# A four-byte tile allocated behind the FFN weights instead of ahead of them

## The chip, the cores and the metric

The kernel runs on one core of a Trainium2 chip. The metric is the device time of one execution in microseconds. The core has a matrix engine (TensorE, PE in the profile, with its weight loads PEld shown apart), a vector engine (VectorE, DVE), a scalar engine (ScalarE, ACT), GpSimd (POOL) and SyncE (SP), which here issues most of the DMA transfers.

## The reference

A transformer layer in two halves on x of shape 4 x 512 x 512, with pre-normalisation and residuals. The first half is an attention that works in the Fourier domain of each of the 16 heads (32 values a head): normalised spectra, a running sum over the positions, a product, and the way back. The second half is a gated FFN (512 to 1536 to 512) whose weights are rounded to 8-bit floats and back.

```python
q = (x @ W_q.T).reshape(B, S, H, hd)
kv = (x @ W_kv.T).reshape(B, S, H, hd)
qf = _l2_normalize_complex(jnp.fft.fft(q, axis=-1))
kvf = _l2_normalize_complex(jnp.fft.fft(kv, axis=-1))
kvf = jnp.cumsum(kvf, axis=1)
values_hat = jnp.fft.ifft(qf * kvf, axis=-1).real
attn = values_hat.reshape(B, S, D) @ W_o.T
...
gate = jax.nn.silu(_quantized_matmul(x, gate_w, gate_scale))
up = _quantized_matmul(x, up_w, up_scale)
return _quantized_matmul(gate * up, down_w, down_scale)
...
x = x + attn_ref(_layernorm(x), W_q, W_kv, W_o)
x = x + ffn_ref(_layernorm(x), gate_w, up_w, down_w, gate_scale, up_scale, down_scale)
```

`_quantized_matmul` multiplies by the weights cast to float8_e4m3 and back, then by a scale.

## The kernel before

The order of every engine's instructions is the order in which the code records them. The work is staged in three.

At the start the attention weights are loaded (`raw`, on SP's queue) and multiplied by the tables of the transform, so that one product of x with the folded weights gives a spectrum: `fold_in` and `fold_out`, into `wkv`, `wq` and `wo`.

Then come 16 chunks of 128 positions, `for i in range(2, N)` with the first two written out ahead of it. A chunk's two spectra (`spectrum`, line 302, tiles `pq`) are f32 matmuls; each of these is two instructions in the profile. `squared` and `summed` (lines 313 and 318) and the power -0.5 on POOL (`norms`, line 323, operands `ss` and `nhalf`) give the norms. `k_scaled` and `k_low` split the scaled values into two fp32r tiles, `kh` and `kl`. The running sum is two fp32r matmuls with the triangle of ones `tri_r` as weights (`running`, line 357, tile `cum`). `products`, `combined`, `v_transpose` and `project` (line 397, tile `po`, f32, with the weights taken from `qvT`) end the chunk. `stats` has another power on POOL (line 259), of the tile `dev`. Between them, `next_parts` rounds the FFN's weights piece by piece; the last of a piece's operations, `quant_sub` (line 225), writes 128 x 1024 elements of `wg`, `wu` or `wd`.

The third stage is the FFN: 48 steps, four batches of 512 rows by 12 blocks of 128 inner columns. In a step, `inner` has 16 fp32r matmuls (line 465): `lhsT`, the weights loaded into the array, is a 128 x 128 block of `wg` or `wu`; `rhs`, streamed through it, is `yh` or `yl`, 512 columns. Their results are the tiles `gu`. ACT and DVE make `fh` and `fl` of them. `down` has 8 fp32r matmuls for an earlier step (line 498, tiles `pd`): here `fh` or `fl` is loaded and 512 columns of `wd` are streamed. In all that is 48 x 24 = 1152 matmuls. Each is preceded by its own load of weights, which the profile shows as LDWEIGHTS on PEld.

Constants lie in the pool `const`, one buffer each, and are placed in SBUF one behind the other in the order of their allocation, each in whole units of 32 bytes per partition. A tile of four bytes so takes 32. The addresses, in bytes within a partition, of the tiles around the change are:

| tile | bytes | address before | past a multiple of 64 |
|---|---|---|---|
| over | 4 | 18592 | 32 |
| table | 4 | 18624 | 0 |
| nhalf | 64 | 18656 | 32 |
| tri_r | 512 | 18720 | 32 |
| wg | 24576 | 19232 | 32 |
| wu | 24576 | 43808 | 32 |
| wd | 24576 | 68384 | 32 |
| gus | 96 | 92960 | 32 |
| dsc | 2048 | 93056 | 0 |

The other tiles lie behind these. All that are matmul operands there start on a multiple of 64: `yh`, `yl`, `fh`, `fl`, `kh`, `kl`, `xT`, `qvT`, `wq`, `wkv`, `wo`. Of the 128 x 1 tiles `less` and `dev`, some start on a multiple of 64 and some 32 bytes past one.

`table` is set to zero on POOL (line 131) and passed through a Silu on ACT (line 132), whose first instruction on ACT is a load of the activation table. Nothing reads `table` afterwards.

Of the kernel before, what the change touches and what calls it, by code (L numbers as in the profile page):

```python
# [7 lines left out]
F32 = mybir.dt.float32  # L8
I32 = mybir.dt.int32
F32R = mybir.dt.float32r  # L10
AF = mybir.ActivationFunctionType
# [4 lines left out]
P = 128  # L16
# [14 lines left out]
def tile_fft_attention_then_fp8_ffn(  # L31
# [38 lines left out]
    nc = tc.nc  # L70
# [9 lines left out]
    const = ctx.enter_context(tc.tile_pool(name="const", bufs=1))  # L80
# [45 lines left out]
    nc.gpsimd.memset(eps, EPS)  # L126
    over = const.tile([P, 1], F32, name="over")
    nc.gpsimd.memset(over, -E4M3_OVERFLOW * DOWN * HUGE)

    table = const.tile([P, 1], F32, name="table")  # L130
    nc.gpsimd.memset(table, 0.0)
    nc.scalar.activation(table, table, AF.Silu)
    nhalf = const.tile([P, H], F32, name="nhalf")
    nc.gpsimd.memset(nhalf, -0.5)
    tri_r = const.tile([P, P], F32R, name="tri_r")
# [1 line left out]
    wg = const.tile([P, KC, FF], F32R, name="wg")  # L137
    wu = const.tile([P, KC, FF], F32R, name="wu")
    wd = const.tile([P, MC, D], F32R, name="wd")
    y_all = dram.tile([B, TC, P, D], F32, name="y_all")  # L140
    xn_all = dram.tile([B, TC, P, D], F32, name="xn_all")

# [609 lines left out]
```

## Time and profile before

| what | us |
|---|---|
| median of 3 runs | 481.35 |
| lowest and highest run | 479.42, 481.39 |
| the profiled execution | 480.92 |
| its span, first to last instruction | 479.1 |
| PE busy | 466.3 |
| DVE busy | 286.4 |
| ACT busy | 214.9 |
| POOL busy | 200.9 |

The span is what the views of the profile divide up; the profiled execution's own time has 1.8 us more, which lie around it. Busy times of different engines overlap. Matmuls are pipelined: one shows some 0.39 us, but the next starts 0.23 us after it, so the cadence is read from the starts, or from the chain of work that ended last, which merges neighbours of one kind and gives the start, the length and the count.

A row of the groups reads: line, engine, operation, output<-inputs by their tiles (buffer numbers left out), shapes, count, busy us and mean ns of one, then idle time before them.

```profile
L465 PE MATMUL gu<-yh,wg 128*128 128x512 f32 x192 | 77.0, 401 | 0.0
...
L498 PE MATMUL pd<-wd,fl 128*128 128x512 f32 x192 | 75.7, 394 | 0.0
```

### The profile page before, as it was taken

Reading aid. Unit: us, or ns where it says so; the run is one execution under the profiler, and the core shown is the slowest. Engines: PE = TensorE matmul, PEld = TensorE weight load, DVE = VectorE, ACT = ScalarE, POOL = GpSimd, SP = SyncE. Lnnn points to the kernel's source line nnn. Section 1 sums busy time; section 2 is a strip of 40 time slices with the busy share of each in tenths; the row PEclk is TensorE's granted clock in tenths of the full one; section 3 lists DMA queues with packets and bytes.
Section 4 is the critical chain, followed back from the end, with each engine's and each line's share of the span. In section 5 each row is a group of like instructions: output and inputs, shape, how many; then the busy total and the mean of one; then the engine's idle time right before and its main releaser. Section 6 shows DMA issues by size and latency. Waiting matters only on the chain.

```text
span 479.1 us, 5013 instructions
## 1 busy us (share of the span) xinstructions
PE 466.3 (97%) x1736; PEld 313.7 (65%) x1736; DVE 286.4 (60%) x399; ACT 214.9 (45%) x418; POOL 200.9 (42%) x134
## 2 busy tenths in 40 slices
PE   6999999999999999999999999999999999999995
PEld 5534454444444445568888888888888888888883
DVE  1558998888998787768898352333433332522225
ACT  3647475655646864315753325533226433222220
POOL 0257999987897986531332140122210021400002
PEclk9999999999999999999999999999999999999999
DMA  8920424342442101424241040430041420200002
GB/s 288 349 66 23 154 86 134 110 148 87 140 154 68 64 22 35 164 91 150 55 100 22 1 175 2 100 77 0 22 155 36 96 46 0 89 0 1 0 0 88
DMA packets 46152, 40.72 MB, mean 85 GB/s; under 512 B 27696, under 2 KB 28080, under 8 KB 46128
## 3 DMA queue, kind: packets, MB, share of 16 engines
q1 hardware_dynamic: 45744, 40.39, 26.9%
q8 instruction: 13, 0.21, 0.2%
q14 instruction: 11, 0.09, 0.1%
q10 hardware_dynamic: 384, 0.03, 0.1%
HBM read 28.85 MB, written 11.53 MB: 84 GB/s over the span
## 4 chain that ended last, share of the span: by engine, by line
PE 77%; DVE 8%; ACT 5%; POOL 4%; DMA 3%; issue 2%; SPq 0%; DVEq 0%; ACTq 0%
PE gu L465 37%; PE pd L498 19%; PE pq L302 12%; PE po L397 6%; POOL rn L323 3%; DMA row<-end 2%; PE pkv L150 1%; PE pt_v L271 1%; ACT sq L313 1%; ACT end L364 1%; DVE ss L318 1%; DVE qm L217 1%; PE pw L165 1%; PE cum L357 1%; DVE qa L221 1%
## 5 line engine op out<-in xcount | busy, mean ns | idle before, releaser
L323 POOL TENSOR_TENSOR rn<-ss,nhalf 128x16 f32<-128x16 f32 x32 | 108.2, 3383 | 22.5 <-DVE ss L318 22.5
L478 DVE SCALAR_TENSOR_TENSOR f<-gu,gus,g 128x512 f32<-128x512 f32 x48 | 36.0, 750 | 114.4 <-PE gu L465 112.9
L465 PE MATMUL gu<-yh,wg 128*128 128x512 f32 x192 | 77.0, 401 | 0.0
L465 PE MATMUL gu<-yh,wu 128*128 128x512 f32 x192 | 76.2, 397 | 0.0
L465 PE MATMUL gu<-yl,wg 128*128 128x512 f32 x192 | 75.8, 395 | 0.0
L498 PE MATMUL pd<-wd,fl 128*128 128x512 f32 x192 | 75.7, 394 | 0.0
L498 PE MATMUL pd<-wd,fh 128*128 128x512 f32 x192 | 75.7, 394 | 0.0
L465 PE MATMUL gu<-yl,wu 128*128 128x512 f32 x192 | 75.7, 394 | 0.0
L481 ACT CAST fh<-f 128x512 fp32r<-128x512 f32 x48 | 29.8, 621 | 90.8 <-DVE f L478 90.8
L302 PE MATMUL pq<-wkv,xT 128*128 128x512 f32 x128 | 57.7, 594 | 0.8 <-DVE xT L294 0.8
L476 ACT ACTIVATE g<-gu,gus 128x512 f32<-128x512 f32 x48 | 33.0, 688 | 55.2 <-PE gu L465 55.2
L397 PE MATMUL po<-wo,qvT 128*128 128x512 f32 x128 | 57.6, 593 | 0.0
L302 PE MATMUL pq<-wq,xT 128*128 128x512 f32 x128 | 57.6, 592 | 0.0
L510 POOL TENSOR_TENSOR o<-o,ys 128x512 f32<-128x512 f32 x14 | 17.7, 1295 | 83.6 <-DVE o L508 83.6
L483 DVE TENSOR_TENSOR fl<-f,fh 128x512 fp32r<-128x512 f32 x48 | 36.2, 755 | 27.0 <-ACT fh L481 26.8
L302 PEld LDWEIGHTS pq<-wkv,xT 128*128 128x128 f32 x128 | 24.1, 190 | 30.6 <-issue 27.5
L465 PEld LDWEIGHTS gu<-yh,wg 128*128 128x128 f32 x192 | 36.0, 188 | 9.3 <-issue 0.5
L465 PEld LDWEIGHTS gu<-yl,wg 128*128 128x128 f32 x192 | 36.0, 188 | 9.2 <-issue 0.5
L498 PEld LDWEIGHTS pd<-wd,fh 128*128 128x128 f32 x192 | 36.0, 188 | 8.9
L498 PEld LDWEIGHTS pd<-wd,fl 128*128 128x128 f32 x192 | 36.0, 188 | 8.8 <-DVE fl L483 0.2
L465 PEld LDWEIGHTS gu<-yl,wu 128*128 128x128 f32 x192 | 36.1, 188 | 8.7
L465 PEld LDWEIGHTS gu<-yh,wu 128*128 128x128 f32 x192 | 36.0, 188 | 8.5
(84 smaller groups left out, 596.4 us busy)
## 6 DMA issues: line engine op xcount, KB each, us to landing
x<-in_x SPq DMA_DIRECT2D x16, 256.0 KB, 2.8
xT<-in_xT SPq DMA_DIRECT2D x16, 256.0 KB, 2.6
y_all<-x SPq DMA_DIRECT2D x16, 256.0 KB, 2.0
ys<-y_all SPq DMA_DIRECT2D x4, 1024.0 KB, 6.8
out<-o SPq DMA_DIRECT2D x16, 256.0 KB, 2.0
rawf<-in_gate_w SPq DMA_DIRECT2D x3, 1024.0 KB, 6.9
rawf<-in_up_w SPq DMA_DIRECT2D x3, 1024.0 KB, 5.4
rawf<-in_down_w SPq DMA_DIRECT2D x3, 1024.0 KB, 6.2
```

Of the source, the lines that this page charges most:

```text
L150: nc.tensor.matmul(pw[i][:, j * P : (j + 1) * P], lhsT=r[:, j, i * P : (i + 1) * P], rhs=fwd, start=True, stop=True,)
L165: nc.tensor.matmul(pw, lhsT=inv, rhs=r[:, j, :], start=True, stop=True)
L302: nc.tensor.matmul(pq, lhsT=xTs[i][:, k, :], rhs=w[:, k, :], start=k == 0, stop=k == KC - 1)
L323: nc.gpsimd.tensor_tensor(rns[i, j], sss.pop((i, j)), nhalf, ALU.pow)
L397: nc.tensor.matmul(po, lhsT=qvT[:, k, :], rhs=wo[:, k, :], start=k == 0, stop=k == KC - 1)
L465: nc.tensor.matmul(p, lhsT=w[:, k, m * P : (m + 1) * P], rhs=v[:, k, :], start=k == 0 and v is yhs[b], stop=k == KC - 1 and v is yls[b],)
L476: nc.scalar.activation(g, pgu[0], AF.Silu, scale=gus[:, 0, m : m + 1])
L478: nc.vector.scalar_tensor_tensor(f, pgu[1], gus[:, 1, m : m + 1], g, ALU.mult, ALU.mult)
L481: nc.scalar.copy(fh, f)
L483: nc.vector.tensor_tensor(fl, f, fh.bitcast(F32), ALU.subtract)
L498: nc.tensor.matmul(pds[b][c], lhsT=v[:, c * P : (c + 1) * P], rhs=wd[:, m, :], start=m == 0 and v is fused[n][0], stop=m == MC - 1 and v i ...
L510: add.tensor_tensor(o, o, ys[b][:, c, :], ALU.add)
```

## The change

The three lines of `table` move from ahead of `nhalf` to behind `wd`. Its 32 bytes are then taken behind the weights: `nhalf`, `tri_r`, `wg`, `wu` and `wd` start 32 bytes lower, at 18624, 18688, 19200, 43776 and 68352, each a multiple of 64. `table` starts at 92928, and `gus` and all that follows stay where they were. On POOL, the memset of `table` comes behind that of `nhalf`. The orders of PE, DVE, ACT and SP stay as they were, and no tile changes its size.

```diff
     over = const.tile([P, 1], F32, name="over")
     nc.gpsimd.memset(over, -E4M3_OVERFLOW * DOWN * HUGE)
+    nhalf = const.tile([P, H], F32, name="nhalf")
+    nc.gpsimd.memset(nhalf, -0.5)
+    tri_r = const.tile([P, P], F32R, name="tri_r")
+
+    wg = const.tile([P, KC, FF], F32R, name="wg")
+    wu = const.tile([P, KC, FF], F32R, name="wu")
+    wd = const.tile([P, MC, D], F32R, name="wd")
 
     table = const.tile([P, 1], F32, name="table")
     nc.gpsimd.memset(table, 0.0)
     nc.scalar.activation(table, table, AF.Silu)
-    nhalf = const.tile([P, H], F32, name="nhalf")
-    nc.gpsimd.memset(nhalf, -0.5)
-    tri_r = const.tile([P, P], F32R, name="tri_r")
-
-    wg = const.tile([P, KC, FF], F32R, name="wg")
-    wu = const.tile([P, KC, FF], F32R, name="wu")
-    wd = const.tile([P, MC, D], F32R, name="wd")
     y_all = dram.tile([B, TC, P, D], F32, name="y_all")
```

More of the change, by code (lines that the diff above doesn't have):

```diff
@@ L128, in tile_fft_attention_then_fp8_ffn @@
     nc.gpsimd.memset(over, -E4M3_OVERFLOW * DOWN * HUGE)
-    table = const.tile([P, 1], F32, name="table")
-    nc.gpsimd.memset(table, 0.0)
-    nc.scalar.activation(table, table, AF.Silu)
     nhalf = const.tile([P, H], F32, name="nhalf")
@@ L139, in tile_fft_attention_then_fp8_ffn @@
     wd = const.tile([P, MC, D], F32R, name="wd")
+    table = const.tile([P, 1], F32, name="table")
+    nc.gpsimd.memset(table, 0.0)
+    nc.scalar.activation(table, table, AF.Silu)
     y_all = dram.tile([B, TC, P, D], F32, name="y_all")
```

## The prediction

> **What bounds the kernel now.** I read the head of the page first, then busy time by stage, then the chain of work that ended last, and then single matmuls in order of time.
>
> ```profile
> span 479.1 us, 5013 instructions
> PE 466.3 (97%) x1736; PEld 313.7 (65%) x1736; DVE 286.4 (60%) x399; ACT 214.9 (45%) x418; POOL 200.9 (42%) x134
> PEclk9999999999999999999999999999999999999999
> PE 77%; DVE 8%; ACT 5%; POOL 4%; DMA 3%; issue 2%; SPq 0%; DVEq 0%; ACTq 0%
> ```
>
> ```profile
> 60.00:132.00 72.00, 72.00 (x200) 34.42 (x201) 64.53 (x92) 43.95 (x84) 63.07 (x33) 1.00 0.36 118
> ...
> 212.00:475.00 263.00, 261.42 (x1118) 209.33 (x1116) 120.45 (x159) 95.06 (x181) 48.86 (x44) 1.00 0.20 53
> ```
>
> The columns of the two stage rows are the stretch, its length, busy time (and count) of PE, PEld, DVE, ACT, POOL, the granted clock, DMA share and GB/s. From 212 to 475 us, the FFN, PE never rests at full clock while DVE is busy 120 of 263 us: the cadence of the FFN's matmuls is the time. The chain gives this cadence:
>
> ```profile
> 214.26 3.73 PE gu L465 x16
> ...
> 454.77 3.73 PE gu L465 x16
> 458.50 1.86 PE pd L498 x8
> 460.36 7.46 PE gu L465 x32
> ```
>
> From 214.26 to 460.36 lie 44 steps of 16 gu and 8 pd matmuls: 246.10 / (44 x 24) = 233.05 ns for each. All 1152 FFN matmuls are fp32r. A plain f32 one is issued as two instructions, 429 ns apart (eight pq matmuls in 3.43 us), which is 214.4 ns for 512 columns if each of the two runs over them twice (an estimate). So an fp32r matmul takes some 18.6 ns more than this f32 pace, and all of these, 1152 x 18.6 = 21.4 us, lie on the path.
>
> **The change part by part.** The bytes. wg, wu, wd and tri_r start 32 bytes past a multiple of 64 before, and on a multiple of 64 after; nhalf moves likewise. Each other operand of these matmuls (yh, yl, fh, fl, kh, kl) stands on a multiple of 64 in both. So before, gu loads shifted weights (wg, wu) and streams unshifted data (yh, yl), while pd loads unshifted weights (fh, fl) and streams shifted data (wd). Every fp32r matmul has exactly one shifted operand, which makes the 18.6 ns suspect: is this the price of the shift? Nothing runs the same matmul in the new place, so I bound it: -21.4 us if all of the excess goes; 0 if none; and upward by the longest step in the trace. The starts of FFN matmuls go in threes, 231, 232 and 237 to 238 ns; if all became the long one, (238 - 233.05) x 1152 = +5.7 us.
>
> Which end is nearest? The trace has stretches without the shift. While a matmul streams, the weights of the next one are loaded. A last gu matmul streams yl (unshifted) while fh (unshifted) is loaded: both operands stand as they will after the change. Likewise the second cum matmul streams kl while qvT is loaded, all unshifted; its own tri_r was loaded before.
>
> ```profile
> 120.80 0.40 PE L357 MATMUL cum<-kl,tri_r 128*128 128x512 f32 x1
> ...
> 121.04 1.02 PE L397 MATMUL po<-wo,qvT 128*128 128x512 f32 x2
> ```
>
> ```profile
> 301.49 0.39 PE L465 MATMUL gu<-yl,wu 128*128 128x512 f32 x1
> 301.73 0.39 PE L498 MATMUL pd<-wd,fh 128*128 128x512 f32 x1
> ...
> 303.36 0.39 PE L498 MATMUL pd<-wd,fl 128*128 128x512 f32 x1
> 303.58 0.39 PE L465 MATMUL gu<-yh,wg 128*128 128x512 f32 x1
> ```
>
> The first column is the start. From last gu to first pd is 0.24 us, from cum kl to po 0.24 us: not 0.215. By the start stamps in ns, the 46 undisturbed gu-to-pd steps have a mean of 230.8, the usual kl-to-po step is 233 to 235; and the opposite case, pd streams shifted wd while shifted wg is loaded, has 230.0 (44 steps). Besides, gu and pd swap the shifted role and keep the same threes. And a load of shifted tri_r begins 110 ns before the next load can, where unshifted transposes follow each other by 109. So fp32r runs at 230 to 238 ns with none, one or both operands shifted. I take 0, the nearest of the three values, and keep -21.4 and +5.7.
>
> [...]
>
> The tri_r matmuls: 32 of them, the same question, at most 32 x 18.6 = 0.6 us, partly under other limits; 0.
>
> The writes of wg, wu and wd (L225) move too, and nhalf, which POOL reads:
>
> ```profile
> L225 DVE SCALAR_TENSOR_TENSOR wg<-qm,qa x6: 1215/1216/1219, 41.3 to 230.0; 128x1024 fp32r<-128x1024 f32 x6
> ...
> L221 DVE SCALAR_TENSOR_TENSOR qa<-qm,rawf x18: 1209/1219/2201, 25.8 to 257.0; 128x1024 f32<-128x1024 f32 x18
> ...
> L323 POOL TENSOR_TENSOR rn<-ss,nhalf x32: 2902/3306/4156, 16.1 to 195.4; 128x16 f32<-128x16 f32 x32
> ```
>
> The three numbers are minimum, median and maximum in ns. A write to shifted wg has 1216 ns, the same form into unshifted qa 1219: 0 for the 18 writes; bounds by the minima, 6 ns x 18 = 0.1 us either way. For L323 the bounds are its own extremes: 32 x (2902 - 3383) = -15.4 us and 32 x (4156 - 3383) = +24.7 us of POOL time, but only 2.7% of the span (13 of 108 us) is on the chain, so -1.9 and +3.0 us. I take 0: the other power on POOL, L259, writes a dev that is shifted in some chunks and not in others, and its undisturbed executions take some 551 ns in both; the spread looks like waiting beside DVE.
>
> What else is moved: one memset on POOL and nothing on PE, DVE, SP or a DMA queue. On ACT the order stays (table load, then the activation on table).
>
> ```profile
> 0.72 1.28 ACT L132 ACT_TABLE_LOAD   x1 [0.72 <-PEq L739]
> ...
> 0.77 0.10 POOL L131 MEMSET table<- 128x1 f32 x1
> 0.80 0.11 POOL L134 MEMSET nhalf<- 128x16 f32 x1
> ...
> 2.01 0.20 ACT L132 ACTIVATE table<-table 128x1 f32<-128x1 f32 x1
> ```
>
> The memset of table now comes behind nhalf's, some 0.03 us later, and ends by 0.91; its reader on ACT starts at 2.01, held by the table load. That load hides it with 1.1 us to spare; without this cover it would cost 0.03 us, and ACT's next work waits until 5.56 for x anyway. Nhalf's first reader comes after 5 us.
>
> **Sum.** The profiled execution took 480.92 us: its span of 479.1 and 1.8 around it. Add 0: 480.9. The median shown is 481.35 with runs from 479.42 to 481.39; I give 481.1, between the two. The case's own range is 479.2 to 483.0, the spread of the runs and the same upward.
>
> **The rivals.**
> Faster, the whole excess: the shift costs all 18.6 ns, and one shifted operand suffices for it. For it: all rows at 214.4 ns have unshifted operands, all at 233 one shifted. Against: the stretches above; it lives only if reads run so far ahead that one step doesn't show the rate. 480.9 - 21.4 = 459.5 us.
>
> Faster, one line: if PE fetched 64 bytes at a time, a matmul would read 33 pieces of its 2048 shifted bytes and 8 of the 512 of weights, or 32 and 9: 41 in both roles, 40 after. That explains why gu and pd are alike. 233.05/41 x 1152 = 6.5 us: 474.4. Against: it wants 227 ns for the 46 unshifted steps and 239 for the 44 with two shifts; they have 230.8 and 230.0.
>
> Slower: weights and stream now begin on the same 64-byte phase, and the load of the next weights collides with the running stream in every matmul of the FFN loop, where the opposite phase let most pass. Price: every step becomes the long one, +5.7, 486.6 us; it decides from 2.1 ns a matmul (2.4 us) on. For it: the recurring long step shows that something does beat against the stream. Against: gu-to-pd and pd-to-gu steps have both operands on the same phase already and are not long. POOL's +3.0 by nhalf ends within this price and gets no chance of its own.
>
> That the change doesn't do what it says can be left out: the allocated addresses of the built program do move.
>
> **How the numbers follow.** No change, 0.42. Whole excess 0.20, one line 0.14, collision 0.24. The chances on both sides of no change are too large to leave either out, so the range goes to the whole excess below, 459.5, and the collision above, 486.6. The unchanged case has 0.01 of its chance beyond half a per cent on either side (0.5%, 2.4 us, is about what a measurement of this kernel can tell from no change). So faster 0.35, within 0.5% 0.40, slower 0.25.
>
> **What would show it.** Right: the step of 16 gu and 8 pd matmuls again takes 5.59 us in the chain, the threes of 231, 232 and 238 stay, L225 and L323 keep their minima. The whole excess: a step of 24 x 214.4 = 5.15 us. One line: 5.46. Collision: 5.7, at full clock. If the FFN loop is as before and the time differs, look at 60 to 201 us, where POOL is busy 63 of 72 us at first, and at L323. The prediction fails by its choice of 0 if those stretches are too short to show the rate of a stream.

## The result, and the profile after

| | before | after |
|---|---|---|
| median of 20 runs each, us | 480.79 | 479.76 |
| lowest and highest, us | 479.42, 481.97 | 478.49, 481.19 |
| span of the profiled execution, us | 479.1 | 477.8 |
| one FFN step (16 gu, 8 pd), ns | 5593.3 | 5573.4 |
| mean gap from gu, from pd, ns | 233.26, 232.63 | 232.97, 230.66 |

The ratio is 0.9982, with a 95% interval of 0.9973 to 0.9991: faster by 0.4 to 1.3 us. That is within the 0.5% that was called no change, but it is not nothing. A gap here and below is the time from the start of one matmul to the start of the next, by the start stamps of the trace in ns; a step is the time from the first gu matmul of one FFN step to that of the next; the steps are means over the undisturbed ones behind 214 us, the gaps over all undisturbed matmuls there, the last 24 of pd included.

The head of the page after the change, and its row of busy time by stage for the FFN:

```profile
span 477.8 us, 5013 instructions
PE 465.8 (98%) x1736; PEld 314.3 (66%) x1736; DVE 285.8 (60%) x399; ACT 214.8 (45%) x418; POOL 200.9 (42%) x134
PEclk9999999999999999999999999999999999999999
```

```profile
212.00:475.00 263.00, 260.00 (x1117) 209.11 (x1115) 121.11 (x159) 95.00 (x181) 49.31 (x43) 1.00 0.19 54
```

Nothing is busy for longer or shorter to speak of; the granted clock is 1.00 as before. PE's last matmul ends 1.4 us earlier, which is the 1.4 us that PE is less busy in this window (261.42 before). The chain shows where this comes from. Four steps from the middle of the FFN, before (first block) and after:

```profile
303.75 3.73 PE gu L465 x16
307.48 1.86 PE pd L498 x8
...
326.12 3.73 PE gu L465 x16
```

```profile
302.95 3.73 PE gu L465 x16
306.67 1.85 PE pd L498 x8
...
325.24 3.73 PE gu L465 x16
```

Before, 303.75 to 326.12 is 22.37 us; after, 302.95 to 325.24 is 22.29. So 0.020 us a step, three quarters of it in pd: by the stamps, the eight pd matmuls go from 1860.8 to 1845.7 ns and the sixteen of gu from 3732.5 to 3727.6. If all 48 steps gain the same (an estimate), that is 48 x 19.9 = 0.96 us: the measured difference of the medians, 1.03, to within its interval. Of the 1.4 us by which PE's last matmul ends earlier, 0.47 had been gained when the first full step began (214.26 before, 213.79 after), but kernels with the same FFN weights as the change began theirs at 213.59 and 214.05 (e1 and e4 below), so this part varies from run to run and is not the change's.

The row of gaps within gu changes too. Before, they went in threes; after, a matmul of `yh` is followed by a long gap and one of `yl` by a short one (means of 237.0 and 228.9 ns; before 233.7 and 232.8):

```profile
303.24 0.40 PE L465 MATMUL gu<-yh,wg 128*128 128x512 f32 x1
303.48 0.39 PE L465 MATMUL gu<-yl,wg 128*128 128x512 f32 x1
303.71 0.40 PE L465 MATMUL gu<-yh,wg 128*128 128x512 f32 x1
303.95 0.39 PE L465 MATMUL gu<-yl,wg 128*128 128x512 f32 x1
304.18 0.40 PE L465 MATMUL gu<-yh,wg 128*128 128x512 f32 x1
```

The other rows that were shown of before:

```profile
0.77 0.11 POOL L130 MEMSET nhalf<- 128x16 f32 x1
0.82 0.10 POOL L138 MEMSET table<- 128x1 f32 x1
```

```profile
0.72 1.28 ACT L139 ACT_TABLE_LOAD   x1 [0.72 <-PEq L739]
2.01 0.20 ACT L139 ACTIVATE table<-table 128x1 f32<-128x1 f32 x1
```

```profile
L225 DVE SCALAR_TENSOR_TENSOR wg<-qm,qa x6: 1214/1216/1219, 42.0 to 229.4; 128x1024 fp32r<-128x1024 f32 x6
...
L323 POOL TENSOR_TENSOR rn<-ss,nhalf x32: 2900/3288/4354, 16.8 to 195.9; 128x16 f32<-128x16 f32 x32
```

The memset of table starts 0.05 us later and its reader again at 2.01, behind the table load. The write of wg keeps its 1216 ns, and the power on POOL its minimum, 2900 against 2902.

### The profile page after: what moved, and what is told of

It reads as the page before. It is cut to its first block, busy times and chain, and to the rows that moved or that the text cites. A ratio compares the mean times of both kernels' runs of the same rounds, so it can differ in the third digit from the quotient of the medians.

```text
span 477.8 us, 5013 instructions
## 1 busy us (share of the span) xinstructions
PE 465.8 (98%) x1736; PEld 314.3 (66%) x1736; DVE 285.8 (60%) x399; ACT 214.8 (45%) x418; POOL 200.9 (42%) x134
## 4 chain that ended last, share of the span: by engine, by line
PE 77%; DVE 9%; ACT 5%; POOL 4%; DMA 3%; issue 2%; SPq 0%; DVEq 0%; ACTq 0%
PE gu L465 37%; PE pd L498 19%; PE pq L302 12%; PE po L397 6%; POOL rn L323 3%; DMA row<-end 2%; PE pkv L150 1%; PE pt_v L271 1%; ACT sq L313 1%; ACT end L364 1%; DVE ss L318 1%; DVE qm L217 1%; PE pw L165 1%; PE cum L357 1%; DVE qa L221 1%
```

## The experiments

For all of them it helps to write down one number for gu and one for pd: the distance, the address of the operand that is loaded less that of the operand that is streamed, modulo 512 bytes. 512 is the size of a loaded block of 128 columns, so within a loop the distance stays what it is while k, m and c run. Before, gu stands at 416 (wg at 19232, yh at 103296) and pd at 160 (fh at 187840, wd at 68384); after, at 384 and 192. Where no ratio is given below, a run's time is that of a single execution, and the argument goes by the steps.

| run | gu, pd at | gu, pd ns | step ns | in units of 6.667 ns | time us | before, beside it |
|---|---|---|---|---|---|---|
| before | 416, 160 | 233.3, 232.6 | 5593.3 | 839 | 480.79 |  |
| after | 384, 192 | 233.0, 230.7 | 5573.4 | 836 | 479.76 |  |
| e1 | 384, 192 | 233.0, 230.7 | 5573.4 | 836 | 480.15 | 481.01 |
| e2 | 384, 160 | 232.5, 232.5 | 5580.3 | 835 and 839 in turn | 480.03 | 481.01 |
| e3 | 352, 192 | 233.6, 230.8 | 5582.9 | 835 and 840 in turn | 480.48 | 481.01 |
| e4 | 384, 192 | 233.0, 230.7 | 5573.4 | 836 | 479.97 | 481.01 |
| e7 | 448, 128 | 229.2, 232.5 | 5526.9 | 829 | 477.30 | 481.65 |
| e8 | 0, 64 | 228.4, 233.1 | 5520.0 | 828 | 477.13 | 481.65 |
| e9 | 384, 0 | 232.5, 229.0 | 5553.3 | 833 | 478.88 | 480.67 |
| e10 | 0, 0 | 229.0, 231.1 | 5513.3 | 827 | 477.46 | 480.67 |
| e11 | 480, 480 | 233.3, 233.4 | 5600.0 | 840 | 480.85 | 480.67 |
| e12 | 0, 192 | 227.9, 229.3 | 5480.0 | 822 | 475.16 | 481.09 |

### e1: the same addresses by another tile

```diff
-    eps = const.tile([P, 1], F32, name="eps")
-    nc.gpsimd.memset(eps, EPS)
...
     wd = const.tile([P, MC, D], F32R, name="wd")
+    eps = const.tile([P, 1], F32, name="eps")
+    nc.gpsimd.memset(eps, EPS)
```

> The tile eps, also four bytes, is allocated and set behind the weights; table stays where it was. The weights, tri_r and nhalf lie at exactly the addresses of the change, while the memset of table stays ahead of nhalf's. Theory A (the addresses alone make the difference): the FFN step of 16 gu and 8 pd matmuls takes 5573 ns as after the change (5593 before), the gaps alternate in gu as after the change, and the time is 0.9 us under before. Theory B (the order of the memsets, or chance in the start of the kernel): 5593 ns, the time of before.

Measured: step 5573.4 ns, gaps as after the change, and 480.15 us against 481.01 of before measured beside it, ratio 0.9982 (0.9969 to 0.9995). The addresses make the whole difference in the step; the place of table's memset makes none.

### e2 and e3: the weights of gu alone, the data of pd alone

Both are shown against the kernel before.

```diff
-    table = const.tile([P, 1], F32, name="table")
-    nc.gpsimd.memset(table, 0.0)
-    nc.scalar.activation(table, table, AF.Silu)
...
+    table = const.tile([P, 1], F32, name="table")
+    nc.gpsimd.memset(table, 0.0)
+    nc.scalar.activation(table, table, AF.Silu)
     wd = const.tile([P, MC, D], F32R, name="wd")
```

> table is allocated between wu and wd: wg and wu (loaded as weights) at a multiple of 64, wd (streamed) 32 past one as before. Theory A1 (the place of the streamed operand counts): gu as after or before (233.0 against 233.3 ns), pd stays at 232.6 ns, step 5588 to 5593 ns. Theory A2 (the place of the loaded weights counts, and pd profits from gu's): pd falls to 230.7 ns without having moved itself, step 5573 ns.

```diff
-    eps = const.tile([P, 1], F32, name="eps")
-    nc.gpsimd.memset(eps, EPS)
-    over = const.tile([P, 1], F32, name="over")
-    nc.gpsimd.memset(over, -E4M3_OVERFLOW * DOWN * HUGE)
...
+    over = const.tile([P, 1], F32, name="over")
+    nc.gpsimd.memset(over, -E4M3_OVERFLOW * DOWN * HUGE)
     wd = const.tile([P, MC, D], F32R, name="wd")
+    eps = const.tile([P, 1], F32, name="eps")
+    nc.gpsimd.memset(eps, EPS)
```

> over is allocated between wu and wd and eps behind wd: wg and wu 32 past a multiple of 64, wd at one. Theory A1 (the place of the streamed operand counts): pd falls from 232.6 to 230.7 ns, gu stays at 233.3 with its threes of 231, 232 and 238; step 5577 ns. Theory A2: pd stays at 232.6, step 5588 to 5593 ns.

Measured: with wd as before, pd keeps 232.5 ns; with wd as after, it falls to 230.8. So pd's gain belongs to wd, which is A1 for pd, and A2 falls. But gu moves a little by itself in both (232.5 and 233.6 ns), and the steps of 5580.3 and 5582.9 ns lie between the expectations: two kinds of step alternate, 5568 and 5592 ns in e2, 5566 and 5600 in e3. So one group's gaps seem to depend on what lies around it. By its addresses e3 isn't quite the half that it was meant to be: with two tiles gone from ahead of them, wg and wu moved by 64 bytes.

### e4: everything shifted

```diff
     dsc = const.tile([P, D], F32, name="dsc")
+    pad = const.tile([P, 1], F32, name="pad")
+    nc.gpsimd.memset(pad, 0.0)
```

> The kernel before with one more tile of 32 bytes behind the constants: the weights stay 32 past a multiple of 64 and every other matmul operand now is too. Theory R (the two operands' place relative to each other counts): they agree, as after the change, so the step takes 5573 ns. Theory S (the distance from a multiple of 64 counts for each operand): all are shifted, none gains, and the step takes 5593 ns or more.

Measured: 5573.4 ns, the means of gu and pd as after the change. Four steps of the chain:

```profile
303.21 3.73 PE gu L465 x16
306.94 1.85 PE pd L498 x8
...
325.50 3.73 PE gu L465 x16
```

303.21 to 325.50 is again 22.29 us. Here the weights stand where they stood before, 32 bytes past a multiple of 64, and all that moved is the rest. Theory S falls: it is not an operand's alignment that counts, but where the weights stand to what moved here.

That is the other operand of each matmul, but also the tiles that ACT, DVE and POOL read and write during the FFN. Their traffic can be left out, as two steps of the kernel before show (the columns are those of the rows by stage):

```profile
236.63:242.22 5.59, 5.59 (x25) 4.50 (x25) 5.59 (x6) 3.18 (x9) 2.27 (x2) 1.00 0.48 104
443.58:449.17 5.59, 5.59 (x25) 4.50 (x25) 1.44 (x3) 1.31 (x2) 0.00 (x0) 1.00 0.00 0
```

DVE is busy for all 5.59 us of the first and for 1.44 of the second, POOL for 2.27 and for nothing, the DMA engines for 0.48 of the time and not at all, and all 43 undisturbed steps take 5592 to 5594 ns. What is left is where the loaded and the streamed operand stand to each other.

### e5: a quarter of the load

```diff
-                for v in (yhs[b], yls[b]):
+                nc.tensor.matmul(
+                    p,
+                    lhsT=w[:, k, m * P : (m + 1) * P],
+                    rhs=yhs[b][:, k, :],
...
+                if k < KC - 1:
                     nc.tensor.matmul(
...
+                        p[:32],
+                        lhsT=w[:, k, m * P : m * P + 32],
+                        rhs=yls[b][:, k, :],
```

> The kernel before, but the gu matmuls that stream yl load 32 columns of weights instead of 128, and the last of these is left out: 96 of each 128 inner columns lack the low parts, so the output differs a little. While yh is streamed, the short load of the next weights runs; while yl is streamed, a full one. Theory L (the load of the next weights collides with the running stream, 20 ns for 128 columns): the gap from a yh matmul to its yl matmul falls from 233 to about 218 ns (213.3 and a quarter of 20), the gap from yl to the next yh stays at 229 to 238. Theory F (fp32r streams 512 columns at this pace whatever is loaded beside it): all gaps stay at 229 to 238.

The loads (minimum, median and maximum in ns), and then single matmuls of one half of a step, by start and length:

```profile
L464 PEld LDWEIGHTS gu<-yh,wg x192: 186/188/192, 195.3 to 444.4; 128*128 128x128 f32 x192
...
L472 PEld LDWEIGHTS gu<-yl,wg x144: 107/108/111, 195.8 to 444.1; 128*32 128x32 f32 x144
```

```profile
302.08 0.39 PE L464 MATMUL gu<-yh,wg 128*128 128x512 f32 x1
302.31 0.40 PE L472 MATMUL gu<-yl,wg 128*32 128x512 f32 x1
302.55 0.39 PE L464 MATMUL gu<-yh,wg 128*128 128x512 f32 x1
302.77 0.39 PE L472 MATMUL gu<-yl,wg 128*32 128x512 f32 x1
303.00 0.39 PE L464 MATMUL gu<-yh,wg 128*128 128x512 f32 x1
```

A short load takes 108 ns, a full one 188. The load beside a yh matmul is short, and its gap has a mean of 231.2 ns (233.7 before); the load beside a yl matmul is full, and its gap has 232.5 (232.8 before). All gu gaps together have a mean of 231.7 ns, against 233.3. Theory L's 218 ns does not appear: a load that is 80 ns shorter took at most some 2.5 ns off the gap, of the 20 that the theory gave to a whole load. (The time, 459.75 us, is that of two matmuls a step fewer.)

### e6: half the columns

```diff
-            for k in range(KC):
-                for v in (yhs[b], yls[b]):
+            for h in (slice(0, S // 2), slice(S // 2, S)):
+                for k in range(KC):
+                    for v in (yhs[b], yls[b]):
...
-                        rhs=v[:, k, :],
...
+                            p[:, h],
+                            lhsT=w[:, k, m * P : (m + 1) * P],
+                            rhs=v[:, k, h],
```

> The kernel before, but each gu matmul is split into two of 256 columns, each with its own load of 128 columns of weights; the result is the same. Theory L (20 ns for each load of 128 columns): 106.7 + 20 = 127 ns a half, so 32 of them in 4.05 us instead of 3.73, and the step takes 5.9 us. Theory F (a pace per streamed column): 116.5 ns a half, the step stays at 5.6 us.

```profile
300.04 3.83 PE gu L466 x32
303.87 1.86 PE pd L499 x8
305.74 3.83 PE gu L466 x32
```

32 halves take 3.83 us, 119.7 ns each; the time is 486.25 us, with a step of 5.70 us. That lies between both theories. The expectations took 213.3 ns as the pace of 512 columns. The rows of before give the same: an f32 instruction of 512 columns starts 429 ns after the last (pq), one of 128 columns 109 ns (the transposes pt_v), so (429 - 109) / 384 = 0.833 ns a column, and 213.3 ns for 512 if such an instruction runs over its columns twice; that it does is an assumption that no run shows, and the 213.3 an estimate by it. A half then stands 13 ns above its 106.7, a whole matmul 20 above 213.3. So by this estimate some 13 ns go with the matmul and not with its columns, and the last 7 ns of the 20 are something that halves mostly avoid. Measured is that two halves take 239.4 ns where a whole matmul takes 233.3.

### e7 and e8: the weights 64 and 128 bytes further

```diff
+    ahead = const.tile([P, 16], F32, name="ahead")
+    nc.gpsimd.memset(ahead, 0.0)
     wg = const.tile([P, KC, FF], F32R, name="wg")
     wu = const.tile([P, KC, FF], F32R, name="wu")
     wd = const.tile([P, MC, D], F32R, name="wd")
+    rear = const.tile([P, 112], F32, name="rear")
+    nc.gpsimd.memset(rear, 0.0)
```

This is e7, against the changed kernel; e8 has 32 and 96 columns in place of 16 and 112.

> The changed kernel with a tile of 64 bytes ahead of wg and one of 448 behind wd: wg, wu and wd move by 64 bytes against all other operands, and stay on multiples of 64. Theory M64 (only the operands' distance modulo 64 counts): step 5573 ns, as after the change. Theory M128 (a longer period counts): another step, and gu, whose distance was a multiple of 128 and now isn't, changes places with pd, whose wasn't and now is: gu 230.7 and pd 233 ns, step 5555 ns.

> The same with 128 bytes ahead of wg and 384 behind wd. Theories M64 and M128: step 5573 ns and the same row of gaps as after the change. Theory M256 or longer: another step or row of gaps.

Measured: 5526.9 and 5520.0 ns, 477.30 and 477.13 us (one run each; before had 481.65 beside them, also one run). M64 and M128 fall: the distance counts with a period of more than 128 bytes. In e8 gu falls to 228.4 ns while pd, at 64, has 233.1. Its single matmuls show what a favourable distance looks like:

```profile
304.09 0.39 PE L469 MATMUL gu<-yl,wu 128*128 128x512 f32 x1
304.32 0.39 PE L469 MATMUL gu<-yh,wu 128*128 128x512 f32 x1
304.55 0.39 PE L469 MATMUL gu<-yl,wu 128*128 128x512 f32 x1
304.77 0.39 PE L469 MATMUL gu<-yh,wu 128*128 128x512 f32 x1
305.00 0.39 PE L469 MATMUL gu<-yl,wu 128*128 128x512 f32 x1
```

Four gaps in 0.91 us; by the stamps, after six matmuls gu settles at 227, 227, 226 ns, again and again, where before the change it went 231, 232, 237. The sum of three is 680 instead of 700 ns: each matmul is 6.7 ns shorter, as much as halves avoid by the estimate above. That both are the same thing is not shown.

### e9, e10 and e11: is there one curve for the distance?

All three are the changed kernel with unread tiles ahead of wg, between wu and wd and behind wd, 512 bytes together; e9 for one:

```diff
     wu = const.tile([P, KC, FF], F32R, name="wu")
+    between = const.tile([P, 48], F32, name="between")
+    nc.gpsimd.memset(between, 0.0)
     wd = const.tile([P, MC, D], F32R, name="wd")
+    rear = const.tile([P, 80], F32, name="rear")
+    nc.gpsimd.memset(rear, 0.0)
```

> The changed kernel with 192 bytes between wu and wd and 320 behind wd: wg and wu at the addresses of the change, wd 192 bytes further, all other operands 512 further. Theory D (what counts is the distance from the streamed operand to the one loaded beside it, modulo 512, by one curve for gu and pd: at a distance of 0, 64, 128, 192, 224, 352, 384, 448 bytes a matmul has had 228.4, 233.1, 232.5, 230.7, 232.6, 233.3, 233.0, 229.2 ns): gu keeps its distance of 384 and its 233.0 ns; pd goes from 192 to 0 and from 230.7 to some 228.4 ns; step 5555 ns. Theory E (gu and pd have curves of their own, or the period is longer than 512 bytes): pd anything from 226 to 238, or gu off 233.

> 128 bytes ahead of wg, 64 between wu and wd, 320 behind wd. By theory D both gu and pd stand at a distance of 0: 228.4 ns each or a little less, since the beginning of each group no longer comes from another phase: step 5440 to 5482 ns, 5.3 to 7.4 us under before, some 474.5 us. Theory E: gu 228.4 as it had at this distance, pd anything, step 5460 to 5560 ns.

> 96 bytes ahead of wg, 128 between wu and wd, 288 behind wd: gu and pd both at a distance of 480, between 448 (229.2 ns) and 0 (228.4). Theory D with a smooth curve: 227 to 230 ns for both, step 5450 to 5520 ns. If multiples of 64 matter beside the distance over 512 (as the step from 192 to 224 had it for pd, 230.7 to 232.6): 231 to 233 ns, step 5545 to 5590 ns.

Two distances in these texts are wrong: the entries 352 and 224 belong to the kernel before and should read 416 and 160.

Measured: e9 agrees with theory D in pd (229.0 ns for 228.4) and in the step (5553 for 5555). e10 does not: gu has its 229.0, but pd, at the distance that gave 229.0 in e9, has 231.1; the step of 5513 ns is off D's 5440 to 5482, and the time is 477.46 us against 480.67 (ratio 0.9933, 0.9920 to 0.9947). The addresses of wd (68544) and of fh (188352) are the same in both runs, so no longer period explains it either: one curve for each matmul by itself is not enough. e11 lies between two good distances of gu (448 in e7, 0 in e8) and is the slowest of all, 5600 ns. It has an odd multiple of 32, as both groups had before the change. All groups at odd multiples of 32 (both of before, pd in e2, gu in e3, both here) have 232.5 to 233.6 ns; those at multiples of 64 have from 227.9 to 233.1.

### e12: the two best parts together

```diff
+    ahead = const.tile([P, 32], F32, name="ahead")
+    nc.gpsimd.memset(ahead, 0.0)
     wg = const.tile([P, KC, FF], F32R, name="wg")
     wu = const.tile([P, KC, FF], F32R, name="wu")
+    between = const.tile([P, 96], F32, name="between")
+    nc.gpsimd.memset(between, 0.0)
     wd = const.tile([P, MC, D], F32R, name="wd")
```

> 128 bytes ahead of wg, 384 between wu and wd, none behind: gu at a distance of 0 as in the runs with 128 bytes, pd at 192 as after the change, both against operands that stand 512 further. If gu and pd each keep the gap that their own distance gave alone (228.4 and 230.7 ns): step 5500 ns, 4.5 us under before, and the fastest version so far. If the phase that one group leaves behind sets the gaps of the next, as the run with both at a distance of 0 suggests: another sum, 5510 to 5560 ns.

Measured: 475.16 us against 481.09, ratio 0.9870 (0.9851 to 0.9890), the fastest of all. Its chain:

```profile
302.35 3.65 PE gu L469 x16
306.00 1.83 PE pd L502 x8
307.83 3.65 PE gu L469 x16
```

The step of 5480 ns is better than either expectation: pd has 229.3 ns here and had 230.7 at the same distance behind a gu of 384. The distance from wd to fh is the same in both to the byte, 119488. So what lies around a group acts on it, and here to the good. It can be the other group's distance, or the seam: while the last pd matmul streams wd, the first block of wg is loaded (before, the matmul starts at 303.36 us and so does the load), and this pair has a distance of its own. It is 0 before, after and in e1, e4, e7 and e8, but 480 in e2 and e3, 320 in e9, 448 in e10, 384 in e11 and 128 in e12. No run changes the seam alone. (5593.3 - 5480.0) x 48 = 5.4 us of the 5.9 measured.

## Why the prediction was right, and where its steps were off

**The bound.** Right: all that the change did, and all that the experiments gained, lies in the cadence of the FFN's matmuls, to within the intervals (by the steps 0.96 of the 1.03 us, and in e12 5.4 of 5.9).

**"I take 0."** The forecast, no change within 0.5%, held, since what the shift moves is small: -0.96 us in the FFN where 0 was taken. The term was mis-sized by 0.8 ns a matmul. The evidence for it was too coarse for that. It put the gaps with no operand shifted (230.8 ns), with both (230.0) and with one (231 to 238) down as one range, 230 to 238, though 2 ns a matmul are 2.3 us. Its own signs of being right did not all come: the step takes 5.57 us and not again 5.59, and the threes of 231, 232 and 238 are gone from gu. That the forecast held is in part luck: the addresses do count, this move of 32 bytes just happened to change little, and with 64 bytes more (e7) the step is 66 ns shorter than before, 3.2 us over 48 steps and more than the half per cent.

**"With none, one or both operands shifted."** This looked at the right pairs and asked a wrong question of them. The gu-to-pd pair with none shifted and the pd-to-gu pair with both have distances that are multiples of 64 (64 and 0), and they were the two lowest rows; the kl-to-po step, at 256, has 233 to 235 ns all the same. e4 shows that it is the distance that counts. And the stretches were single matmuls between longer groups, whose gaps differ with what lies around them (pd at distance 0 has 229.0 ns in e9 and 231.1 in e10; at 192, 230.7 after the change and 229.3 in e12): the prediction named this as the way it would fail, and a single gap indeed did not show what a run of them does, 230.8 ns with no operand shifted where gu, with none shifted, has 233.0 after the change.

**The whole excess, 459.5 us.** Wrong, as the prediction held more likely: no distance that was tried brings a matmul near 214 ns. That pace rests on the same assumption as the 213.3 at e6, two passes over the columns, which no run shows. The lowest that a group settles at is 226.7 ns (e8, e12), and by the estimate at e6 some 13 ns above the estimated time of the columns stay even with half of them.

**One line, 474.4 us.** Wrong for this change: the step lost 19.9 ns, not 136 (24 matmuls at 5.7 ns). But these 5.7 ns are near what favourable distances do take off, 6.7 ns a matmul, and the best layout reaches 475.2 us; nothing shows that this is more than chance. Its account by pieces read falls with e4, where the same operands, all shifted, behave as after.

**The collision, 486.6 us.** Its sign was wrong. It held that operands on the same 64-byte phase collide; but all odd multiples of 32 that were tried are slow (232.5 to 233.6 ns; before, and e11 as the slowest), and of the multiples of 64 some are fast and some slow (227.9 to 233.1). That something beats against the stream is not shown; that the long gaps are no fixed part of the cadence is: in e8 gu settles at 227, 227, 226 ns, without the 237 of before.

**The rest.** The memset behind the table load, the writes of L225 and the power on POOL cost nothing that shows, as worked out; e1 has the same addresses with table's memset ahead of nhalf's, and the same step.

That 32 bytes count at all is measured: 19.9 ns a step by the change, and from e11 to e12, which differ only in the place of the weights among unread tiles, 5600 to 5480 ns.

What stays open: whether 13 ns go with each fp32r matmul, as the estimate at e6 has it, and what they are; what meets what when the distance is unfavourable (a collision of two reads is a guess that e4 allows and no run shows); the period of the distance, of which only more than 128 bytes is shown, so that the 512 of the table are a convention; and whether a group is changed by the distance in the other or by the seam between them.

## What to carry to other kernels

Where a loop of matmuls is the bound, read the cadence of its matmuls from the starts, and try the place of the operands in SBUF against each other as a cheap setting: here a change of addresses alone is worth 1.3%. Moving a small tile moved all that is allocated between its two places, so a kernel can gain or lose some tenths of a per cent (0.2% here) by an edit that has nothing to do with its matmuls. To judge such an effect read the exact starts over a whole step of the loop, not a few single gaps.

## What was not expected of the hardware

In all these kernels but e5 and e6, the undisturbed FFN step has a mean that is a whole number of 6.667 ns to within 0.3 ns (839, 836, 829, 828, 833, 827, 840, 822), or, in e2 and e3, alternates between two such numbers to within 2 ns. At the best distance, in e8 and e12, an fp32r matmul of 512 columns settles at 34 of these units (226.7 ns), in gu before the change at 35 (233.3). And the kernels repeat these patterns from step to step, and from one kernel to the next where the distances agree: after the change, e1 and e4 have the same 5573.4 ns by three different edits.
